# The tail of an attention and mixture-of-experts layer: first terms of the sums, additions and the last scaling placed elsewhere

## The chip, the cores and the metric

The kernel runs on one core of a Trainium2 chip. The metric is the device time of one execution in microseconds, from the first to the last instruction of the program with what lies around it. Without the profiler, three runs of the kernel before gave 538.71, 541.92 and 542.86 us; their median is 541.92 us. Its engines are named as in the profile: PE is TensorE's matmul, PEld its weight load, DVE is VectorE, ACT is ScalarE, POOL is GpSimd, SP is SyncE, which here only starts DMAs.

## The reference

The input x has 8 sequences of 512 tokens of 128 numbers, all float32. Two steps follow each other, each with a residual and a layer norm without scale and offset:

```python
x = _layernorm(x + attention(x))        # 16 heads of 8, causal, softmax
x = _layernorm(x + ffn(x))              # 14 experts, two for each token

# ffn, for one token:
#   w1, w2 = softmax of the token's logits, its two highest, made to sum to 1
#   out_k  = gelu(x @ W1[e_k] + b1[e_k]) @ W2[e_k] + b2[e_k]
#   result = clip(x + w1 * out_1 + w2 * out_2, -100, 100)

def _layernorm(x, eps=1e-05):
    m = mean(x); v = var(x)
    return (x - m) / sqrt(v + eps)
```

The part of the computation that this change touches is the very end: for each token the sum of x, its weighted biases and the two expert results, the clip, the residual, and the second layer norm.

## The kernel before

Tokens lie on 128 partitions. A sequence is four blocks of 128 tokens (`NQ` = 4), so a tensor for one sequence is 128 x 512 numbers; there are 8 sequences (`B`).

The kernel goes through these stages. Attention runs over 32 units (sequence and group of four heads) in a software pipeline written out by hand: a table of jobs gives each step its list of calls, so the order of instructions on each engine is the order in which the program issues them. Each engine works through its own list in order and waits on semaphores where an instruction needs another engine's result. While attention goes on, each finished sequence is routed: the two experts of each token are found, and GpSimd scatters the token's row, with its weight and its number, into the rows of those experts in a DRAM tensor, `XS`. Then the experts' blocks of 256 or 128 rows are loaded, multiplied through both layers, weighted, and scattered by GpSimd to `OS`, a DRAM tensor with two rows for each token (one for the first and one for the second expert). Between expert blocks, `biases(c)` (L1166) puts into `acc` what each token of sequence c has so far: its normalised input `y_sb` plus its weighted second-layer biases. `acc` and `z_sb` are the same memory as `x_sb`, the kernel's input, which is no longer needed.

The tail begins at L1242. It works sequence by sequence.

- `gather(c)` (L1245) starts two DMAs of 256 KB, one on SyncE's queue and one on ScalarE's, which bring the two expert rows of each token of sequence c back from `OS`. Six sequences are started at once; the buffers (`bufs=6`) of the first two are used again for sequences 6 and 7, as soon as TensorE has read them. The first gather waits for all scatters.
- `add_up(c)` (L1254) adds three terms in a PSUM bank by multiplying each with the identity matrix: first `acc`, then the two gathered tiles. The bank comes from the pool `ps_m`, which has two. The first sum's first term stands directly behind the last expert's matmuls in TensorE's queue; each later one stands behind the sum before it.
- `residual_2(c)` (L1260) clips the sum (L1263, VectorE, from PSUM to SBUF), adds `y_sb` (L1264, VectorE), and takes mean and variance of each of the four blocks (L220 and L221, VectorE, four pairs). `layernorm_scale` (L223) then gives scale and shift with four small GpSimd instructions: epsilon to the variance (L228), the power of -0.5 (L229), mean times scale (L230), and the sign (L231).
- `store(c)` (L1269) scales and shifts the four blocks with four ScalarE instructions (L1273) and starts one DMA of 256 KB to the output from SyncE's queue (L1281).

The loop at L1287 issues, for c from 0 to 9, `add_up(c)` and `residual_2(c)`, the gather six sequences ahead, and `store(c - 2)`. On VectorE the tail is thus, for each sequence in turn, one clip, one addition and four pairs of statistics instructions. Two other lines are named later because their instructions resemble new ones: L675, an addition of two 128 x 512 tiles by GpSimd in the attention part, and L770, a comparison on VectorE in the routing.

Of the kernel before, what the change touches and what calls it, by code (L numbers as in the profile page):

```python
# [8 lines left out]
FP = mybir.dt.float32  # L9
AF = mybir.ActivationFunctionType  # L10
ALU = mybir.AluOpType
# [4 lines left out]
P = 128  # L16
# [10 lines left out]
LN_EPS = 1e-5  # L27
# [9 lines left out]
def kernel(  # L37
# [18 lines left out]
    nc = tc.nc  # L56
    B, T, D = x.shape
    E, _, F = w1.shape
    NQ = T // P
# [28 lines left out]
    out_v = out.rearrange("b (t p) d -> p (b t) d", p=P)  # L88
# [8 lines left out]
    ident = const.tile([P, P], FP, tag="ident", name="ident")  # L97
# [61 lines left out]
    power = const.tile([P, NQ], FP, tag="power", name="power")  # L159
# [52 lines left out]
    y_sb = const.tile([P, NT, PW], FP, tag="y_sb", name="y_sb")  # L212
    nc.gpsimd.tensor_copy(y_sb[:, :, D + 1], ids[:, 0, :])
    stats = const.tile([P, NT, 2], FP, tag="stats", name="stats")
# [3 lines left out]
    def layernorm_stats(pool, src, t):  # L218
        st = pool.tile([P, nc.vector.BN_STATS_DIM], FP, tag="bn", name=f"bn_{t}", bufs=4)
        nc.vector.bn_stats(st, src)  # L220
        nc.vector.bn_aggr(stats[:, t, :], st)  # L221

    def layernorm_scale(pool, c, n):  # L223

        ts = slice(c * NQ, (c + 1) * NQ)
        rstd = pool.tile([P, NQ], FP, tag="rstd", name=f"rstd_{n}_{c}")
        shift = pool.tile([P, NQ], FP, tag="shift", name=f"shift_{n}_{c}")
        nc.gpsimd.tensor_scalar(rstd, stats[:, ts, 1], LN_EPS, 1.0, ALU.add, ALU.mult)  # L228
        nc.gpsimd.tensor_tensor(rstd, rstd, power, ALU.pow)  # L229
        nc.gpsimd.tensor_tensor(shift, stats[:, ts, 0], rstd, ALU.mult)  # L230
        nc.gpsimd.tensor_scalar(shift, shift, -1.0, 0.0, ALU.mult, ALU.add)  # L231
        return rstd, shift
# [23 lines left out]
    def after_scatters(inst, those):  # L256
        for s in those:
            tc.add_manual_dep(
                inst.ins,
                s.name,  # L260
                mybir.DependencyInfo(mybir.DependencyClass.Sync, mybir.DependencyReason.DATA),
                reason="reads what they wrote",
            )
# [9 lines left out]
    with tc.tile_pool(name="work", bufs=2) as work, tc.tile_pool(  # L273
        name="scratch", bufs=2, space=bass.MemoryType.DRAM
    ) as scratch, tc.tile_pool(
        name="ps_m", bufs=2, space=bass.MemoryType.PSUM
# [10 lines left out]
        def bank(name, dt=FP):  # L287
            return ps_m.tile([P, 2048 // mybir.dt.size(dt)], dt, tag="bank", name=name)
# [80 lines left out]
        def split(step, b, w, bias, nm):  # L369

            ps = bank(f"{nm}_{b}")
            nc.tensor.matmul(ps, w, xTs[b], start=True, stop=True)
            pc = work.tile([P, PC, T], BF, tag=f"{nm}pc", name=f"{nm}pc_{b}", bufs=1)
            nc.scalar.activation(pc[:, 0, :], ps, AF.Identity, bias=bias)
            rest = work.tile([P, T], FP, tag=f"{nm}rest", name=f"{nm}rest_{b}", bufs=1)
            nc.vector.scalar_tensor_tensor(
                rest, ps, bias, pc[:, 0, :], op0=ALU.add, op1=ALU.subtract
            )

            sc = scratch.tile([NG * HD, PC, GH, T], BF, tag=f"{nm}sc", name=f"{nm}sc_{b}")  # L380
            pieces[nm, b] = sc

            def store(cs):
                for c in cs:
                    nc.sync.dma_start(sc[:, c].rearrange("d j t -> d j t"), pc[:, c, :])

            def others():
                nc.scalar.copy(pc[:, 1, :], rest)
                nc.vector.tensor_tensor(pc[:, 2, :], rest, pc[:, 1, :], ALU.subtract)

            if step < 0:
                others()
                store(range(PC))
            else:
                at(step + 1, others)
                at(step + 1, store, (0,))
                at(step + 2, store, (1, 2))
# [104 lines left out]
        avs, pts, outs, sums = {}, {}, {}, {}  # L502
# [463 lines left out]
        def step_of(u, i):  # L966
            return u * UN + i
# [25 lines left out]
        for u in range(NU):  # L993
            b, g = divmod(u, NG)
            f, k = step_of(u, 0), step_of(u, 0) + LAG
# [148 lines left out]
        while s < NU * UN + LAG + 1 or s + 1 in jobs:  # L1144
# [5 lines left out]
            for fn, args in jobs.pop(s, ()):  # L1150
                fn(*args)
        held.close()
        ffn = held.enter_context(tc.tile_pool(name="ffn", bufs=3, reuse_waits="tile"))
# [3 lines left out]
                    name=n, bufs=2, space=bass.MemoryType.PSUM, reuse_waits="tile"  # L1157
# [6 lines left out]
        acc = z_sb = x_sb  # L1164
# [78 lines left out]
        got, sums, scales = {}, {}, {}  # L1243

        def gather(c):  # L1245
            got[c] = []
            for k, eng in enumerate((nc.sync, nc.scalar)):
                o = ffn.tile([P, NQ, D], FP, tag=f"o{k}", name=f"o{k}_{c}", bufs=6)
                inst = eng.dma_start(o, out_k[k][:, c * NQ : (c + 1) * NQ, :])
                if c == 0:  # L1250
                    after_scatters(inst, scatters["OS"])
                got[c].append(o)

        def add_up(c):  # L1254
            sums[c] = bank(f"sum_{c}").rearrange("p (t d) -> p t d", d=D)
            parts = acc[:, c * NQ : (c + 1) * NQ, :], *got.pop(c)
            for i, part in enumerate(parts):
                nc.tensor.matmul(sums[c], ident, part, start=(i == 0), stop=(i == 2))

        def residual_2(c):  # L1260
            ts = slice(c * NQ, (c + 1) * NQ)
            z = z_sb[:, ts, :]
            nc.vector.tensor_scalar(z, sums.pop(c), CLIP, -CLIP, ALU.min, ALU.max)  # L1263
            nc.vector.tensor_tensor(z, z, y_sb[:, ts, 0:D], ALU.add)  # L1264
            for i in range(NQ):
                layernorm_stats(ffn, z_sb[:, c * NQ + i, :], c * NQ + i)
            scales[c] = layernorm_scale(ffn, c, 1)

        def store(c):  # L1269
            rstd, shift = scales.pop(c)  # L1270
            for i in range(NQ):
                t = c * NQ + i
                nc.scalar.activation(  # L1273
                    z_sb[:, t, :],
                    z_sb[:, t, :],
                    AF.Identity,
                    bias=shift[:, i : i + 1],
                    scale=rstd[:, i : i + 1],
                )
            ts = slice(c * NQ, (c + 1) * NQ)  # L1280
            nc.sync.dma_start(out_v[:, ts, :], z_sb[:, ts, :])  # L1281

        inner.close()
        ffn = inner.enter_context(tc.tile_pool(name="tail", bufs=3, reuse_waits="tile"))
        for c in range(6):
            gather(c)
        for c in range(B + 2):  # L1287
            if c < B:
                add_up(c)
                residual_2(c)  # L1290
                if c + 6 < B:
                    gather(c + 6)
            if c >= 2:
                store(c - 2)


# [41 lines left out]
```

## Time and profile before

| What | Time |
|---|---|
| Median of three runs | 541.92 us |
| The profiled execution | 572.89 us |
| its span, from the first to the last instruction | 571.2 us |
| Last scatter's instruction ends on GpSimd | 530.6 us |
| First gathers start | 532.0 us |
| First sum complete, first clip starts | 539.6 us |
| Second clip starts | 542.9 us |
| Last statistics end | 564.2 us |
| Last scaling ends on ScalarE | 567.9 us |

Places in the profiled execution are given in microseconds from the start of its span; the profiled execution is slower than the runs, and a difference worked out in it is compared with its own time. In the timeline, a row is the start, the duration, the engine, the line in the code, the operation, the tile written and the tile read, and how often; in brackets stands how long the engine sat idle before, and what ended that. In the chain of waits, a row is the start, the share of time that the chain spends there, and the instruction. In a table by windows, each row has the window, its length, the busy time of PE, PEld, DVE, ACT and POOL with the number of instructions, then the granted TensorE clock (1.00 is full speed), the DMA engines' share and GB/s.

From 543 to 564 us VectorE is busy 19.59 of 21 us, TensorE 15.60, ScalarE 10.63 and GpSimd 11.15.

### The profile page before, as it was taken

The page shows a single profiled execution, that of the slowest core. Times are in us where ns is not written, and L with a number is a line of the kernel's source. Part 1 is how long each engine was busy: PE and PEld are TensorE (multiplying, and loading weights), DVE is VectorE, ACT ScalarE, POOL GpSimd, SP SyncE. Part 2 cuts the span into 40 slices and gives each one's busy share as a digit, 9 for nine tenths or more (in the row PEclk, how much of TensorE's full clock was granted, in tenths as well). Part 3 has the DMA queues.
Part 4 walks back from the last instruction along what each step waited for, and adds up shares of the span by engine and source line. Part 5 has one row for each costly group of instructions (what it writes and reads, how often), then busy time and mean ns, then how long its engine had stood idle before and what let it go on. Part 6 is the DMA issues. An engine that isn't in the chain of part 4 may idle for free.

```text
span 571.2 us, 10861 instructions
## 1 busy us (share of the span) xinstructions
PE 462.0 (81%) x3367; PEld 284.3 (50%) x3367; DVE 379.0 (66%) x932; ACT 307.5 (54%) x512; POOL 322.6 (56%) x678
## 2 busy tenths in 40 slices
PE   1757999999999899999999998777658787776491
PEld 0433655555555555445455554446546666665240
DVE  4239577779799798887888989517546344444194
ACT  0303677677677678658666474566224345444044
POOL 6001343545786785786876777636746545656153
PEclk9997799999999999999999999699669889989696
DMA  6153324434534535434344253322433212221763
GB/s 178 61 153 112 104 72 135 136 104 136 167 127 134 165 105 151 156 130 143 127 156 139 68 157 99 115 70 75 136 107 99 67 55 71 77 58 41 199 164 89
DMA packets 66739, 66.23 MB, mean 116 GB/s; under 512 B 10860, under 2 KB 55381, under 8 KB 66682
## 3 DMA queue, kind: packets, MB, share of 16 engines
q1 hardware_dynamic: 55008, 53.26, 31.3%
q0 software_dynamic: 4512, 8.47, 4.5%
q10 hardware_dynamic: 7162, 3.81, 2.5%
q8 instruction: 27, 0.44, 0.3%
q14 instruction: 30, 0.25, 0.2%
HBM read 37.75 MB, written 26.05 MB: 112 GB/s over the span
## 4 chain that ended last, share of the span: by engine, by line
PE 44%; DVE 21%; ACT 11%; issue 7%; DMA 6%; POOL 5%; another core or an unknown queue 3%; ACTq 1%; SPq 1%; DVEq 0%; POOLq 0%
PE av L587 10%; PE f L423 7%; PE b L509 6%; ACT pt L563 6%; PE h L1102 4%; PE o L1119 4%; PE f L433 2%; DVE ob L1127 2%; DVE mx L463 2%; DVE mx L468 2%; POOL pt L520 2%; PE bp L1177 2%; ACT oT L597 2%; DVE mx L475 2%
## 5 line engine op out<-in xcount | busy, mean ns | idle before, releaser
L563 ACT ACTIVATE pt<-b 128x1024 f32<-128x1024 f32 x160 | 162.8, 1021 | 44.7 <-PE b L509 30.6
L520 POOL TENSOR_SCALAR_AFFINE_SELECT pt<-pt 128x256 f32<-128x256 f32 (+1 forms) x210 | 91.6, 451 | 74.6 <-ACT pt L563 73.7
L423 PE MATMUL f<-ring 72*128 72x384 bf16 (+3 forms) x512 | 114.4, 307 | 17.8 <-DMA ring<-qsc 8.2
L243 POOL DMA_INDIRECT OS<-ob,bto_i x77 | 75.0, 974 | 62.4 <-DVE ob L1127 45.7
L509 PE MATMUL b<-ring 75*128 75x384 bf16 (+3 forms) x512 | 100.2, 307 | 6.8 <-ACT pt L563 3.4
L475 DVE TENSOR_REDUCE mx<-f 128x2 f32<-128x1024 f32 x64 | 78.1, 1223 | 29.1 <-PE f L433 27.1
L587 PE MATMUL av<-pt,v_aug 128*32 128x512 f32 (+3 forms) x1024 | 84.8, 443 | 4.8 <-POOL pt L520 4.2
L433 PE MATMUL f<-causal_bf,ident_bf 128*128 128x256 bf16 (+1 forms) x320 | 82.5, 258 | 0.0
L468 DVE TENSOR_REDUCE mx<-f 128x8 f32<-128x1024 f32 x64 | 77.1, 1214 | 5.6 <-PE f L433 5.3
L423 PEld LDWEIGHTS <-ring 72*128 72x128 bf16 x512 | 50.7, 100 | 52.1 <-issue 28.4
L1107 ACT ACTIVATE hT<-h,wt 128x256 f32<-128x256 f32 (+1 forms) x92 | 35.2, 436 | 61.6 <-PE h L1102 31.5
L509 PEld LDWEIGHTS <-ring 75*128 75x128 bf16 x512 | 42.4, 99 | 39.7 <-issue 27.5
L1119 PE MATMUL o<-wt,hT 128*128 128x128 f32 x308 | 48.0, 300 | 8.2 <-ACT hT L1107 7.5
L587 PEld LDWEIGHTS av<-pt,v_aug 128*32 128x32 f32 x1024 | 27.2, 109 | 51.9 <-issue 38.6
L1102 PE MATMUL h<-bxT,wt 128*128 128x256 f32 (+1 forms) x184 | 46.9, 382 | 6.9 <-ACT wt L1074 3.3
L1119 PEld LDWEIGHTS o<-wt,hT 128*128 128x128 f32 x308 | 45.3, 212 | 12.7 <-ACT hT L1107 9.1
L1127 DVE TENSOR_SCALAR ob<-o,bxb 128x128 f32<-128x128 f32 x77 | 24.1, 347 | 40.6 <-PE o L1119 14.7
L463 DVE TENSOR_REDUCE mx<-f 128x4 f32<-128x1024 f32 x32 | 39.1, 1223 | 16.0 <-PE f L433 11.8
L1102 PEld LDWEIGHTS h<-bxT,wt 128*128 128x128 f32 x184 | 33.0, 215 | 14.0 <-issue 6.7
L433 PEld LDWEIGHTS <-ident_bf 128*128 128x128 bf16 x320 | 31.7, 99 | 14.8 <-issue 2.3
L243 POOL DMA_INDIRECT XS<-y_sb,to_i x32 | 32.3, 1010 | 9.4 <-issue 5.6
L243 POOL DMA_INDIRECT XS<-second,to_i x32 | 32.4, 1012 | 8.9 <-issue 8.9
(215 smaller groups left out, 630.2 us busy)
## 6 DMA issues: line engine op xcount, KB each, us to landing
ring<-ksc SPq DMA_DIRECT2D x32, 288.0 KB
ring<-qsc SPq DMA_DIRECT2D x96, 96.0 KB
osc<-oT SPq DMA_DIRECT2D x24, 256.0 KB
bxb<-XS SPq DMA_DIRECT2D x31, 130.0 KB
ring<-in_L_ffn_w_dram SPq DMA_DIRECT2D x28, 128.0 KB
qsc<-qpc SPq DMA_DIRECT2D x24, 128.0 KB
ksc<-kpc SPq DMA_DIRECT2D x24, 128.0 KB
x_sb<-in_L_attn_x_dram SPq DMA_DIRECT2D x8, 256.0 KB
```

What stands on the lines that cost most here:

```text
L243: inst = nc.gpsimd.indirect_dma_start(dst, bass.IndirectOffsetOnAxis(ap=idx, axis=0), src, None, bounds_check=bound, oob_is_err=False,)
L423: nc.tensor.matmul(ps[:, col : col + W], qr[u % RING][0:KR, j, qb * P : (qb + 1) * P], kr[u % RING][0:KR, j, :W], start=first, stop=False, ...
L433: nc.tensor.matmul(out, ident_bf, causal_bf[:, 0:n, :], start=False, stop=True, skip_group_check=True,)
L463: nc.vector.reduce_max(mx[:, :, 5], ps.rearrange("p b (s k) -> p (b s) k", s=2), axis=AX.X)
L468: nc.vector.reduce_max(mx[:, j : j + 2, 1:5], ps.rearrange("p b (s k) -> p b s k", k=P), axis=AX.X,)
L475: nc.vector.reduce_max(mx[:, j : j + 2, 7], ps, axis=AX.X)
L509: nc.tensor.matmul(ps[:, col : col + W], kr[u % RING][:, j, kb * P : (kb + 1) * P], qr[u % RING][:, j, kb * P :], start=first, stop=True, ...
L520: nc.gpsimd.affine_select(out=view, in_=view, pattern=[[0, k] for k in n] + [[1, P]], compare_op=ALU.is_ge, fill=0.0, base=0, channel_mult ...
L563: nc.scalar.activation(pt, ps, AF.Exp, scale=SCALE)
L587: nc.tensor.matmul(avs[u][HS * j : HS * (j + 1), kb * P :], v_aug[b % 2][:, kb, g * GH + j, :], p, start=(kb == 0), stop=(kb == 2),)
L1102: nc.tensor.matmul(hp[:, f, :], wt[:, f * P : (f + 1) * P], xT, start=True, stop=True)
L1119: nc.tensor.matmul(op[:, s, :], hT[:, f, s * P : (s + 1) * P], wt[:, F + f * D : F + (f + 1) * D], start=(f == 0), stop=(f == NFC - 1),)
```

## The change

The tail's functions are taken apart and issued in another order, and some of their work is given to other engines.

- The first terms of the sums (`begin_sum`) are issued apart from the other two (`add_up`). They go into a pool of their own, `ps_t`, with six PSUM banks. Six first terms are issued with the first six gathers. Those of sequences 6 and 7 follow the clips of sequences 0 and 1, whose banks they use again; in TensorE's queue they stand ahead of the remaining terms of sequences 1 and 2.
- The addition of `y_sb` is GpSimd's for sequences 0 to 6, and VectorE's for the last one.
- Epsilon is added to the variance by VectorE. GpSimd takes only the power. The shift (minus mean times scale) is one VectorE instruction.
- The order on VectorE is: clip of c, shift of c-2, statistics of c-1, variance plus epsilon of c-1. The last sequence's addition and statistics stand ahead of the shift of the seventh.
- For the last sequence, two blocks are scaled by VectorE and stored from SyncE's queue, and two are scaled by ScalarE and stored from ScalarE's queue.

```diff
+        def begin_sum(c):
+            sums[c] = ps_t.tile([P, NQ, D], FP, tag="sum", name=f"sum_{c}")
+            nc.tensor.matmul(
+                sums[c], ident, acc[:, c * NQ : (c + 1) * NQ, :], start=True, stop=False
+            )
+
         def add_up(c):
-            sums[c] = bank(f"sum_{c}").rearrange("p (t d) -> p t d", d=D)
-            parts = acc[:, c * NQ : (c + 1) * NQ, :], *got.pop(c)
-            for i, part in enumerate(parts):
-                nc.tensor.matmul(sums[c], ident, part, start=(i == 0), stop=(i == 2))
+            for i, part in enumerate(got.pop(c)):
+                nc.tensor.matmul(sums[c], ident, part, start=False, stop=(i == 1))
 
-        def residual_2(c):
+        def clip(c):
             ts = slice(c * NQ, (c + 1) * NQ)
             z = z_sb[:, ts, :]
             nc.vector.tensor_scalar(z, sums.pop(c), CLIP, -CLIP, ALU.min, ALU.max)
-            nc.vector.tensor_tensor(z, z, y_sb[:, ts, 0:D], ALU.add)
+
+            if c < B - 1:
+                nc.gpsimd.tensor_tensor(z, z, y_sb[:, ts, 0:D], ALU.add)
+
+        def measure(c):
+            ts = slice(c * NQ, (c + 1) * NQ)
+            if c == B - 1:
+                z = z_sb[:, ts, :]
+                nc.vector.tensor_tensor(z, z, y_sb[:, ts, 0:D], ALU.add)
             for i in range(NQ):
                 layernorm_stats(ffn, z_sb[:, c * NQ + i, :], c * NQ + i)
-            scales[c] = layernorm_scale(ffn, c, 1)
+            rstd = ffn.tile([P, NQ], FP, tag="rstd", name=f"rstd_1_{c}")
+            nc.vector.tensor_scalar(
+                rstd, stats[:, ts, 1], LN_EPS, 1.0, ALU.add, ALU.mult
+            )
+            nc.gpsimd.tensor_tensor(rstd, rstd, power, ALU.pow)
+            scales[c] = rstd
+
+        def move(c):
+            ts = slice(c * NQ, (c + 1) * NQ)
+            shift = ffn.tile([P, NQ], FP, tag="shift", name=f"shift_1_{c}")
+            nc.vector.scalar_tensor_tensor(
+                shift, stats[:, ts, 0], -1.0, scales[c], op0=ALU.mult, op1=ALU.mult
+            )
+            scales[c] = scales[c], shift
 
         def store(c):
             rstd, shift = scales.pop(c)
...
+            for half, eng in enumerate((nc.sync, nc.scalar)):
+                for i in range(2 * half, 2 * half + 2):
+                    t = c * NQ + i
+                    z = z_sb[:, t, :]
+                    if c == B - 1 and half == 0:
+                        nc.vector.tensor_scalar(
+                            z, z, rstd[:, i : i + 1], shift[:, i : i + 1], ALU.mult, ALU.add
+                        )
+                    else:
+                        nc.scalar.activation(
...
+                if c == B - 1:
+                    ts = slice(c * NQ + 2 * half, c * NQ + 2 * half + 2)
+                    eng.dma_start(out_v[:, ts, :], z_sb[:, ts, :])
+            if c < B - 1:
+                ts = slice(c * NQ, (c + 1) * NQ)
+                nc.sync.dma_start(out_v[:, ts, :], z_sb[:, ts, :])
 
         inner.close()
         ffn = inner.enter_context(tc.tile_pool(name="tail", bufs=3, reuse_waits="tile"))
+        ps_t = inner.enter_context(
+            tc.tile_pool(
+                name="ps_t", bufs=6, space=bass.MemoryType.PSUM, reuse_waits="tile"
+            )
+        )
+
         for c in range(6):
             gather(c)
+            begin_sum(c)
         for c in range(B + 2):
             if c < B:
                 add_up(c)
-                residual_2(c)
+                clip(c)
                 if c + 6 < B:
                     gather(c + 6)
-            if c >= 2:
+                    begin_sum(c + 6)
+            if c == B:
+                measure(c - 1)
+            if c > 1:
+                move(c - 2)
                 store(c - 2)
+            if 1 <= c < B:
+                measure(c - 1)
```

More of the change, by code (lines that the diff above doesn't have):

```diff
@@ L1269, in store @@
+        def move(c):
[5 more added lines that the diff above has]
+            scales[c] = scales[c], shift
         def store(c):
             rstd, shift = scales.pop(c)
[L1271 to L1279, printed above, removed]
@@ L1280, in store @@
-            ts = slice(c * NQ, (c + 1) * NQ)
-            nc.sync.dma_start(out_v[:, ts, :], z_sb[:, ts, :])
+            for half, eng in enumerate((nc.sync, nc.scalar)):
[8 more added lines that the diff above has]
+                        nc.scalar.activation(
+                            z,
+                            z,
+                            AF.Identity,
+                            bias=shift[:, i : i + 1],
+                            scale=rstd[:, i : i + 1],
+                        )
+                if c == B - 1:
+                    ts = slice(c * NQ + 2 * half, c * NQ + 2 * half + 2)
+                    eng.dma_start(out_v[:, ts, :], z_sb[:, ts, :])
@@ L1283 @@
+            if c < B - 1:
+                ts = slice(c * NQ, (c + 1) * NQ)
+                nc.sync.dma_start(out_v[:, ts, :], z_sb[:, ts, :])
         inner.close()
         ffn = inner.enter_context(tc.tile_pool(name="tail", bufs=3, reuse_waits="tile"))
+        ps_t = inner.enter_context(
+            tc.tile_pool(
+                name="ps_t", bufs=6, space=bass.MemoryType.PSUM, reuse_waits="tile"
+            )
+        )
         for c in range(6):
             gather(c)
+            begin_sum(c)
```

## The prediction

> **What bounds the kernel now.** The change touches only what follows the last expert block, so I read the chain of waits in order of time from there.
>
> ```profile
> 531.98 3.76 DMA o<-OS
> 535.78 7.12 PE sum L1258 x10
> 542.92 0.70 DVE x_sb L1263
> ...
> 543.65 0.70 DVE x_sb L1264
> ...
> 564.68 1.02 POOL rstd L229
> ```
>
> The tail is in three parts: the first gather is awaited until 535.78 us; TensorE adds up the first sums, at half clock, until 542.9; then VectorE alone sets the pace. Its chain repeats every 3.03 us (clip at 546.07 and at 549.10) to the last sequence. TensorE, ScalarE and GpSimd wait beside it: ScalarE sat idle 29.6 us before its scalings, behind GpSimd's shift. Next, the timeline of the same stretch, for the hand-over to GpSimd and the end.
>
> ```profile
> 543.25 1.04 POOL L229 TENSOR_TENSOR rstd<-rstd,power 128x4 f32<-128x4 f32 x1
> 543.65 0.69 DVE L1264 TENSOR_TENSOR x_sb<-x_sb,y_sb 128x512 f32<-128x512 f32 x1
> ...
> 564.06 0.18 DVE L221 BATCH_NORM_AGGREGATE stats<-bn 128x2 f32<-128x6 f32 x1
> 564.40 0.19 POOL L228 TENSOR_SCALAR rstd<-stats 128x4 f32<-128x4 f32 x1 [1.19 <-DVE stats L221]
> ...
> 566.27 1.65 ACT L1273 ACTIVATE x_sb<-x_sb,shift,rstd 128x128 f32<-128x128 f32 x4 [1.38 <-POOL shift L231]
> ```
>
> A power costs GpSimd 1.01 to 1.04 us for four columns. Now it lies beside VectorE's next sequence, and nothing on VectorE waits for it: shift and its sign are GpSimd's too. ScalarE ends at 567.92; the last store and the end of the program take until 571.2, another 3.28.
>
> **What moves off VectorE.** The addition of y, 0.69 us (0.72 to the next start), leaves VectorE for seven of eight sequences. Two small instructions come: the variance with epsilon (nearest row L944, 176 ns) and the shift, a scalar_tensor_tensor on four columns (nearest L782, 162 ns); each delays its successor by about 0.10. If nothing waited, a round would be 0.60 (clip) + 0.10 + 1.51 (first bn to last aggregate, 544.37 to 545.88) + 0.20 + 0.10 = 2.51 us instead of 3.03.
>
> **The wait that comes in.** The order on VectorE becomes: clip of c, shift of c-2, statistics of c-1, variance of c-1. The shift reads the power, and the power starts only when the variance, the instruction just before the clip, is done. Only the clip covers it. From the variance's start (call it R): 0.17 for itself, 0.10 to GpSimd, 1.01 for the power, 0.03 back, so the shift starts at R+1.31; the clip frees VectorE at R+0.70. VectorE stands 0.6 us each round, with the statistics of the next sequence queued behind the shift, and ScalarE behind these. Round: 1.31 + 0.17 - 0.08 (a successor starts that much before the end) + 1.51 + 0.20 = 3.11 us. That alone eats the whole gain. The 0.10 lies between 0.08 (149.51 to 149.59 below) and 0.16 (564.24 to 564.40).
>
> **What the moved addition does.** GpSimd's queue becomes: power of c-2, addition of c, power of c-1. The clip of c is done by R+0.8, so the addition of c is ready to go when the power ends. The trace of before has this addition's like (x plus bias) and the two hand-overs:
>
> ```profile
> 149.10 0.20 POOL L787 TENSOR_SCALAR w<-gap 128x4 f32<-128x4 f32 x1
> 149.33 0.18 DVE L788 RECIPROCAL w<-w 128x4 f32<-128x4 f32 x1 [1.34 <-POOL w L787]
> 149.59 0.20 POOL L789 TENSOR_TENSOR w<-gap,w 128x4 f32<-128x4 f32 x1 [0.30 <-DVE w L788]
> 149.73 0.19 POOL L790 COPY y_sb<-w 128x4 f32<-128x4 f32 x1
> ...
> 333.94 1.27 POOL L675 TENSOR_TENSOR xb<-x_sb,bo_bc 128x512 f32<-128x512 f32 x1
> 333.98 1.31 DVE L770 TENSOR_TENSOR hot<-rank,best 128x56 f32<-128x56 f32 x1
> ```
>
> VectorE starts 0.03 after GpSimd's result (149.30 to 149.33). A GpSimd instruction that needs nothing of the one before starts 0.06 before that one's end (149.73 against 149.79). So the addition starts 0.09 ahead of the shift. And L770, which takes 0.22 us elsewhere, took 1.31 when it started 0.04 behind such an addition, and ended 0.08 after it. It reads two operands from SBUF; so does the shift (mean and rstd). L817, also two operands, lasts 0.36 instead of 0.27 each time it starts 0.14 behind a short GpSimd product. The Trainium skill ("SBUF — State Buffer", section "SBUF: two separate sides") says why: VectorE and GpSimd share a pair of ports under an exclusive lock; a VectorE instruction with two SBUF inputs and a GpSimd instruction exclude each other for the whole instruction. The power rows above speak against the "whole": L1264, with two inputs, ran its usual 0.69 in the middle of a power. By the rule the powers would also block; by the rows only an instruction that streams many columns does. I follow the rows: the additions block, the powers do not. The shift of c-2 is then held to the end of the addition of c:
>
> R + 0.17 + 0.10 + 1.01 - 0.06 + 1.27 + 0.08 = R+2.57, then -0.08 + 1.51 + 0.20: a round of 4.20 us.
>
> Bounds: no hold, 3.11; hold, 4.20. L770 and the shift differ in columns (56 against 4), but the wait is for the other engine, so I take the hold. The statistics read one operand, and an L477 reduction under L675 took its usual 0.17; they are counted as free of it.
>
> **The first sums.** Six first terms run in the wait, 6 x 0.86 from 525.7, to about 530.9 us (their banks are free once the last expert outputs are evacuated, about 526.4). They take one 0.86 off each sum, but VectorE is the bound after the second sum, and the first sum had its first term early already. Could they keep TensorE's clock up? Windows of 3.41 us on the grid at which the clock changes:
>
> ```profile
> 462.43:465.84 3.41, 0.91 (x9) 0.67 (x7) 0.85 (x5) 1.76 (x4) 1.73 (x3) 1.00 0.33 99
> 465.84:469.26 3.42, 3.21 (x6) 1.90 (x7) 1.22 (x5) 0.00 (x0) 1.91 (x2) 0.50 0.25 77
> ...
> 534.11:537.53 3.42, 1.75 (x2) 0.84 (x3) 0.00 (x0) 0.00 (x0) 0.00 (x0) 0.50 1.14 315
> 537.53:540.94 3.41, 3.41 (x5) 1.35 (x4) 1.31 (x2) 0.00 (x0) 0.00 (x0) 0.50 1.20 291
> ```
>
> The first number after the window's length is TensorE's busy time, the third from the end the granted clock. The Trainium skill ("TensorE: Matmul & The Clock Gate", Part 1) drops the clock after an idle window of about 3.4 us. 530.9 to 535.78 is 4.9 us idle, which holds a whole window in (4.9-3.41)/3.41 = 44% of phases; in the rest the sum would be ready near 537.5 and 2.1 us would be won. But the row of 462.43 lost the clock with 0.91 us of work in its window, and 4.9 us of idle time leave no more than 0.96 in the worse of two windows. I take the clock as lost, and the first sum where it is, 539.6.
>
> The second sum gets later: the seventh first term reuses the first bank and stands ahead of it in TensorE's queue, waiting for the first clip. 539.60 + 0.69 + about 1.1 (partly half clock) + 1.72 puts the second clip at about T = 543.2, against 542.92: +0.3. Before, VectorE used that wait for the first statistics; now these stand behind the second clip.
>
> **The sum.** First variance R0 = T + 0.60 + 1.51 + 0.20 = T+2.31. The third clip waits for the eighth first term (again behind a clip) and its own two terms: T+3.3. It ends after the first power, so this addition comes late and the shift passes ahead of it: R1 = T + 3.32 + 0.60 + 0.09 + 1.71 = T+5.72. Four rounds with the hold: R5 = T+22.52. The last sequence has no GpSimd addition, so one round without: R6 = T+25.63. Then VectorE's own addition and statistics, 0.09 + 0.72 + 1.71: R7 = T+28.15. The seventh sequence's shift stands behind that, so ScalarE scales it from R7+0.29 to R7+1.94 and only then the last two blocks, to R7+2.72. VectorE's half is ready at about R7+2.1 (L904 gives 0.33 and 0.23 more), hidden. From there the 3.28 of before, and an estimated 0.1 for two stores of the same moment: T+34.25 = 577.45. Before: 571.2. That is +6.3 us; the profiled execution would be 572.89 + 6.3 = 579.2. It is longer than the median of the runs by 31 us, but the tail's steps are fixed latencies, so I carry the difference over whole: 541.92 + 6.3 = 548.2.
>
> What is hidden: GpSimd's work (2.28 us a sequence against 1.6, inside the round) and the stores of the first six sequences. The end itself is 0.8 shorter (6.94 to 6.1 after the last variance), counted above.
>
> **Rivals.** (1) The shift gets its operands before the addition takes the ports: 4 x 1.09 less, +1.9, 543.8. For it: L770 is one instance. Against: the start order, and L817's five. (2) Not slower: the power comes back before the clip ends, and the round is 2.51. After R1 five such rounds give R6 = T+18.3 and the end at T+26.9, 1.1 us ahead of before: 540.8. It needs the power and its hand-overs within 0.5 us; all rows say 1.0. (3) Worse: the third round is held too (+1.1), or single-operand statistics are slowed by additions: 550 and above. For it: the third clip's margin is only about 0.4 us.
>
> **Chances.** Forecast 0.60, (1) 0.25, (2) 0.08, (3) 0.07. One per cent, 5.4 us, is about what a measurement of this kernel can tell from no change (its three runs span 4.2). The forecast lies 0.9 us above that bound, so about 0.7 of its chance is on the slower side: 0.52 slower with (3), 0.45 within, 0.03 faster. Range 542.5 (leaves out most of (2)) to 551 (takes in the extra held round).
>
> **What would show it.** Shifts of four columns lasting 1.1 to 1.3 us on VectorE in rounds 3 to 6, each ending with a GpSimd addition; the clip to clip distance 4.2 there; TensorE at half clock at 536; ScalarE's seventh sequence directly ahead of the eighth. Wrong, if shifts last 0.2 with 0.6 us of idle time before them, if the distance is below 3.0, or if the first sum is ready by 538.

## The result

The changed kernel takes 546.86 us (median of six runs, 545.29 to 549.45) against 539.09 for the kernel before (six runs in all, 535.61 to 542.86): the ratio is 1.0157, with a 95% interval of 1.012 to 1.0194. The change makes the kernel about 8 us slower.

The two profiled executions can't be compared from end to end. The first one of the kernel before stood some 30 us longer in the expert stage, ahead of the tail: its first gathers start at 531.98 us, those of the changed kernel at 495.97. A second profile of the kernel before (below) has them at 497.94. So I compare tails, from the start of the first gather to the end of the span:

| | before | changed | difference |
|---|---|---|---|
| first gather to first clip | 7.62 us | 7.56 us | -0.06 |
| first clip to second clip | 3.32 us | 5.38 us | +2.06 |
| second clip to the last variance (before: to where L221's last result could be read) | 21.34 us | 28.49 us | +7.15 |
| from there to the end | 6.94 us | 6.10 us | -0.84 |
| sum | 39.22 us | 47.53 us | +8.31 |

The chain of waits of the changed kernel, in order of time (start, share of time, instruction):

```profile
499.71 3.80 PE sum L1262 x4
...
503.53 0.70 DVE x_sb L1267
...
504.28 2.08 PE sum L1256 x2
506.35 2.53 PE sum L1262 x4
...
508.91 0.70 DVE x_sb L1267
...
515.18 1.03 POOL rstd L1283
516.21 0.02 issue
516.23 1.13 DVE shift L1289
...
519.25 1.03 POOL rstd L1283
520.28 0.02 issue
520.30 1.15 DVE shift L1289
```

Two things are new in it. Between the first and the second clip, TensorE's seventh first term (L1256) stands in the chain, behind the first clip. And in each round from 515 us on, GpSimd's power and VectorE's four-column shift stand in it, which were beside it before. The timeline of the changed kernel shows why a shift of four columns takes over a microsecond:

```profile
515.18 1.02 POOL L1283 TENSOR_TENSOR rstd<-rstd,power 128x4 f32<-128x4 f32 x1 [0.70 <-DVE rstd L1280]
516.17 1.17 POOL L1270 TENSOR_TENSOR x_sb<-x_sb,y_sb 128x512 f32<-128x512 f32 x1
516.23 1.13 DVE L1289 SCALAR_TENSOR_TENSOR shift<-stats,rstd 128x4 f32<-128x4 f32 x1 [0.54 <-POOL rstd L1283]
...
532.93 0.16 DVE L1289 SCALAR_TENSOR_TENSOR shift<-stats,rstd 128x4 f32<-128x4 f32 x1 [0.60 <-POOL rstd L1283]
...
534.88 0.69 DVE L1276 TENSOR_TENSOR x_sb<-x_sb,y_sb 128x512 f32<-128x512 f32 x1
535.12 1.31 POOL L1283 TENSOR_TENSOR rstd<-rstd,power 128x4 f32<-128x4 f32 x1 [2.22 <-DVE rstd L1280]
```

GpSimd's addition starts at 516.17, 0.06 us ahead of the shift, and the shift ends at 517.36, 0.02 after it. VectorE stood idle 0.54 for the power before that. Where no addition follows the power (532.93), the shift takes 0.16. Four shifts are held; the clips of their rounds and the next one start at 515.01, 519.08, 523.23, 527.43 and 531.64, 4.07 to 4.21 us apart.

### The profile page after: what moved, and what is told of

It is laid out like the page before. It is cut to its first block, busy times and chain, and to the rows that moved or that the text cites. A ratio compares the mean times of both kernels' runs of the same rounds, so it can differ in the third digit from the quotient of the medians.

```text
span 543.5 us, 10853 instructions
## 1 busy us (share of the span) xinstructions
PE 448.6 (83%) x3367; PEld 276.0 (51%) x3367; DVE 382.3 (70%) x943; ACT 306.0 (56%) x510; POOL 325.8 (60%) x661
## 4 chain that ended last, share of the span: by engine, by line
PE 49%; DVE 17%; ACT 12%; DMA 7%; POOL 6%; issue 6%; ACTq 1%; SPq 1%; DVEq 0%; POOLq 0%
PE av L587 12%; PE f L423 8%; PE b L509 7%; ACT pt L563 7%; PE o L1119 5%; PE h L1102 4%; PE f L433 3%; POOL pt L520 2%; DVE mx L468 2%; DVE mx L463 2%; ACT oT L597 2%; DMA OS<-ob,bto_i 2%; PE bp L1177 2%; ACT x_sb L1305 2%; DVE ob L1127 2%
## 5 line engine op out<-in xcount | busy, mean ns | idle before, releaser
L1102 PE MATMUL h<-bxT,wt 128*128 128x256 f32 (+1 forms) x184 | 43.7, 361 | 5.6 <-DVE begins L873 3.3
L1119 PE MATMUL o<-wt,hT 128*128 128x128 f32 x308 | 43.5, 282 | 1.3 <-ACT hT L1107 1.3
L1119 PEld LDWEIGHTS o<-wt,hT 128*128 128x128 f32 x308 | 41.7, 197 | 4.2 <-ACT hT L1107 2.1
L1102 PEld LDWEIGHTS h<-bxT,wt 128*128 128x128 f32 x184 | 30.4, 198 | 11.1 <-ACT wt L1074 5.4
```

Source lines behind the costliest of these rows:

```text
L1102: nc.tensor.matmul(hp[:, f, :], wt[:, f * P : (f + 1) * P], xT, start=True, stop=True)
L1119: nc.tensor.matmul(op[:, s, :], hT[:, f, s * P : (s + 1) * P], wt[:, F + f * D : F + (f + 1) * D], start=(f == 0), stop=(f == NFC - 1),)
```

## The experiments

All tails below are from one profile each, from the start of the first gather to the end; ratios are to the kernel before on the same chip. They are worked out from the single runs of both, and differ by up to 0.24% from the quotient of the two medians.

| Run | tail, us | median, us | before, us | ratio, 95% interval |
|---|---|---|---|---|
| kernel before, twice | 39.2, 39.4 | | | |
| changed, twice | 47.5, 48.4 | 546.9, 548.8 | 539.1, 540.7 | 1.0157 (1.012 to 1.0194), 1.0128 (1.0055 to 1.0202) |
| the addition waits for the shift | 43.9 | 548.3 | 539.6 | 1.0175 (1.0124 to 1.0226) |
| additions on VectorE | 42.6 | 544.3 | 539.6 | 1.0111 (1.0053 to 1.0169) |
| later first terms | 45.1 | 546.4 | 539.6 | 1.0135 (1.0085 to 1.0184) |
| quarter addition | 45.2 | 547.1 | 539.6 | 1.0150 (1.0104 to 1.0196) |
| first terms alone | 40.5 | 543.1 | 540.7 | 1.0044 (1.0021 to 1.0068) |
| before, clock kept | 37.5 | 538.1 | 540.7 | 0.9947 (0.9920 to 0.9974) |
| changed, clock kept | 44.3 | 544.3 | 538.0 | 1.0117 (1.0070 to 1.0163) |
| changed, both mended | 40.4 | 539.5 | 538.0 | 1.0034 (1.0014 to 1.0053) |
| clip by two engines | 35.5 | 536.7 | 540.7 | 0.9912 (0.9887 to 0.9937) |
| clip by two, second form | 32.9 | 532.0 | 538.0 | 0.9882 (0.9839 to 0.9924) |

### The changed kernel once more

> The changed kernel once more, as the measure for the runs beside it. The profiles give 47.5 us from the first gather's start to the end for it, 39.2 for the kernel before: 8.3 us more. If the shorter tails of the four runs before this one are the whole difference, this one is the slowest of all against the kernel before, by 8 us (547.5); if something ahead of the tail differs between executions and chips, the difference lies anywhere between 6 and 11 us while the tail in the profile is again 47.5.

The tail of this second profile is 48.4 us, four shifts are held for 1.13 us, and the first two clips (506.41 and 512.23) are 5.82 apart. The medians differ by 8.1 us. Both losses, the held shifts and the late second sum, are thus in both profiles of the changed kernel.

### The held shift: one wait more

```diff
-            if c < B - 1:
-                nc.gpsimd.tensor_tensor(z, z, y_sb[:, ts, 0:D], ALU.add)   # in clip(c)
...
             if c > 1:
                 move(c - 2)
+            if c < B - 1:
+                add_y(c, moved.get(c - 2))   # the addition, with a wait for that shift
+            if c > 1:
                 store(c - 2)
```

`add_y` (not shown) is the same addition, which also waits for the shift that it is given.

> The changed kernel with one wait more: GpSimd's addition of sequence c also waits for VectorE's shift of sequence c-2, so it can no longer start ahead of it; nothing else moves. If the additions hold the shifts (forecast's theory), the four shifts of 1.13 us last 0.16 again, the rounds shrink from 4.2 to 3.1 us, and the kernel gains 4 x 1.09 = 4.4 us: about 542.5, and 43 us from the first gather's start to the end instead of 47.5. If the shift is long for a reason of its own (the power's result arriving late, a slow form of instruction), the rounds stay at 4.2 or grow and the time stays at 546.9 or above.

All eight shifts last 0.15 or 0.16 us, the rounds from the fourth clip on are 3.10 to 3.24, and the tail is 43.9 us, 3.6 less than the changed kernel's. A wait was added and the tail got shorter, so the shift's length is the addition's doing. The time without a profile didn't follow: the profiled execution took 543.45 us, the three others 547.4 to 550.1; 542.5 was expected. The pair with the clock kept, below, repeats the test.

### The held shift: dose and response

```diff
-                nc.gpsimd.tensor_tensor(z, z, y_sb[:, ts, 0:D], ALU.add)
+                nc.gpsimd.tensor_tensor(
+                    z[:, 0:1, :], z[:, 0:1, :], y_sb[:, c * NQ : c * NQ + 1, 0:D], ALU.add
+                )
```

> The changed kernel with GpSimd's additions cut to the first of the four blocks of a sequence (the residual is left out for the other three blocks of sequences 0 to 6). Dose and response: if the shift is held exactly as long as the addition runs, an addition of about 0.4 us gives shifts of 0.35 to 0.4 us instead of 1.13, rounds of 3.35 and 3.5 us less in all: 543.4. If the hold is a fixed cost of two engines meeting, the shifts stay near 1.1 us.

The timeline of this run, at the first held shift:

```profile
516.99 1.02 POOL L1285 TENSOR_TENSOR rstd<-rstd,power 128x4 f32<-128x4 f32 x1 [1.42 <-DVE rstd L1282]
517.99 0.45 POOL L1270 TENSOR_TENSOR x_sb<-x_sb,y_sb 128x128 f32<-128x128 f32 x1
518.04 0.41 DVE L1291 SCALAR_TENSOR_TENSOR shift<-stats,rstd 128x4 f32<-128x4 f32 x1 [0.54 <-POOL rstd L1285]
```

An addition of 0.45 us gives a shift of 0.41; all four are 0.41. The hold lasts as long as the addition. Each held shift is 0.72 shorter, which makes 2.9 us; the expected 3.5 was too large. The tail is 2.4 us shorter than the changed kernel's, because in this profile the first clip comes 0.26 us later after the first gather (7.82) and the second 0.19 later after the first (5.57). My 0.35 to 0.4 for the shift was near. The median is 547.1 us and not 543.4: here too the time without a profile didn't follow.

### The additions back on VectorE

```diff
-            if c < B - 1:
-                nc.gpsimd.tensor_tensor(z, z, y_sb[:, ts, 0:D], ALU.add)
+            nc.vector.tensor_tensor(z, z, y_sb[:, ts, 0:D], ALU.add)
...
```

> The changed kernel with the additions of y back on VectorE, directly behind the clips; all the rest as changed. Forecast's theory: no addition on GpSimd, so no hold; clip and addition together (1.3 us) now cover the power's round trip (1.31 us), so the 0.6 us of waiting goes as well and is replaced by the 0.7 us of the addition: rounds of 3.2 us, about 543, 43.5 us of tail. If the waiting for the power were the whole loss and no hold existed, moving the addition back would win nothing: 547.

The rounds are 3.20 to 3.28 us, the shifts 0.15 to 0.16 with no idle time before them: clip and addition cover the power's way to GpSimd and back. The tail is 42.6 us. VectorE does more work than in the changed kernel and is done sooner. Part of the 5 us by which the tail is shorter than the changed kernel's is the clock: here the second clip came 3.63 after the first. The median is 544.3 us; 543 was expected.

### The late second sum: the seventh first term moved

```diff
                 if c + 6 < B:
                     gather(c + 6)
-                    begin_sum(c + 6)
+                if 3 <= c < 5:
+                    begin_sum(c + 3)
```

> The changed kernel with the first terms of sequences 6 and 7 issued three and three sequences later, so that no first term that waits for a clip stands ahead of the second and third sum in TensorE's queue. Theory: the second sum was late (5.4 us after the first, 3.3 before the change) because TensorE stood idle for the clip and so stayed at half clock for another window. Then the second clip comes about 3 us sooner, 2.2 to 2.5 us after the first; but the third clip is then early too, so the shift of the first sequence is held by an addition as the others are (+0.8): together about -2.4, 544.5, tail 45. If the half clock has nothing to do with the wait, only the wait and the matmuls go, about 0.8 + 0.9 us, and with the added hold the time stays within 1 us of 546.9.

The second clip starts 2.07 us behind the first (506.99 and 509.06), and the first sequence's shift is now held too, 1.15 us. The tail is 45.1, as expected. So the seventh first term, its wait for the first clip and what they do to the clock made the second sum late; the half clock's part is the next test. The median is 546.4 us, where 544.5 was expected: no faster than the changed kernel, as far as the noise lets one tell.

### The late second sum: half clock

TensorE's windows in the changed kernel, on the grid at which the clock changes (length, busy time of PE, and near the end the granted clock):

```profile
497.69:501.11 3.42, 1.40 (x2) 0.84 (x3) 0.00 (x0) 0.00 (x0) 0.00 (x0) 0.50 1.08 300
501.11:504.52 3.41, 2.63 (x4) 0.58 (x3) 0.69 (x1) 0.00 (x0) 0.21 (x1) 0.50 1.19 291
504.52:507.93 3.41, 3.41 (x5) 1.35 (x6) 0.00 (x0) 0.00 (x0) 0.96 (x1) 0.51 1.20 290
507.93:511.35 3.42, 2.64 (x7) 0.98 (x6) 2.27 (x10) 0.00 (x0) 1.18 (x1) 1.00 1.17 287
```

(The clock changes about 0.1 us ahead of the edges shown, which leaves the 2.63 as it is.) The second of these windows is busy for 2.63 us of 3.41; the other 0.78 is the wait for the first clip. The clock stayed at half for one window more, and most of the first term and of the second sum ran in it.

Where the windows fall differs from one execution to the next. Six profiles have this opening without further matmuls. In four (the changed kernel twice, the run with the wait, the quarter addition) the whole wait lay inside one window, which was busy for 2.63 or 2.64 us, and the second clip came 5.38 to 5.82 us after the first. In the run with the additions on VectorE the clock was back at 503.65, ahead of the wait; in the run with the first terms alone (below) it came back at 504.85, in the middle of the wait, after a window that was busy for 2.70 us. In these two the second clip came 3.63 and 3.62 after the first. So the loss is frequent, but not certain.

To test the half clock, six matmuls into an unused bank follow the first terms, so that the clock is still full when the gathers land:

```diff
         for c in range(6):
             gather(c)
             begin_sum(c)
+        idle = bank("idle").rearrange("p (t d) -> p t d", d=D)
+        for i in range(6):
+            nc.tensor.matmul(idle, ident, acc[:, 0:NQ, :], start=True, stop=True)
```

> The changed kernel with six matmuls into an unused bank behind the six first terms, so that TensorE is busy until shortly before the first gathers land. Theory: the second sum's delay (5.4 to 5.8 us behind the first instead of the 3.6 that were forecast) is half clock kept up by the wait for the first clip. At full clock it comes 3.3 us behind the first, and the first about 1.5 to 2 us sooner: tail 47.5 - 2.1 - 1.5 = 43.9, about 4 us less than the changed kernel, 544. The four held shifts of 1.13 us stay. If the delay is the wait for the clip itself, only the first sum comes sooner: tail 46.

The timeline of this run:

```profile
503.77 0.69 DVE L1267 TENSOR_SCALAR x_sb<-sum 128x512 f32<-128x512 f32 x1 [11.72 <-PE sum L1262]
...
504.52 1.12 PE L1256 MATMUL sum<-x_sb,ident 128*128 128x512 f32 x2 [0.78 <-DVE x_sb L1267]
...
505.48 1.88 PE L1262 MATMUL sum<-o,ident 128*128 128x512 f32 x4
...
507.40 0.69 DVE L1267 TENSOR_SCALAR x_sb<-sum 128x512 f32<-128x512 f32 x1 [2.94 <-PE sum L1262]
```

Clip to clip is 3.63 us (3.3 expected); the first clip comes 6.09 us after the first gather's start instead of 7.56. Both come sooner at full clock, with the wait for the clip still there, so the half clock was the larger part of the delay; the tail is 44.3 (43.9 expected). The 3.6 that I had forecast for the changed kernel is the distance at full clock.

### Both mended

The same six matmuls, and the additions wait for the shifts.

> The changed kernel with the clock kept as in the run beside it, and with the additions waiting for the shifts, so that both costs are away: no shift over 0.2 us, rounds of 3.1 to 3.2. The tail is 43.9 - 3.6 = 40.3, 3.6 us less than beside it, about 540. If the time without a profile doesn't follow the tail (as in the run with the wait alone), it stays at 544.

```profile
512.03 1.02 POOL L1280 TENSOR_TENSOR rstd<-rstd,power 128x4 f32<-128x4 f32 x1 [0.63 <-DVE rstd L1277]
513.08 0.16 DVE L1294 SCALAR_TENSOR_TENSOR shift<-stats,rstd 128x4 f32<-128x4 f32 x1 [0.54 <-POOL rstd L1280]
...
513.32 1.18 POOL L1285 TENSOR_TENSOR x_sb<-x_sb,y_sb 128x512 f32<-128x512 f32 x1 [0.27 <-DVE shift L1294]
```

Now the shift goes first and the addition follows it. The tail is 40.4 us, 3.9 less than with the hold, and here the runs follow: 539.5 against 544.3, 4.8 less on the same chip. So the hold costs about 4 us of the kernel's time. The fair comparison is with the kernel before with its clock kept too (37.5, below): 2.9 us are left. The first two clip distances are 3.63 and 3.62 us instead of 3.13 and 3.03, with a first term's wait for a clip in each: 1.1 us. From the fourth clip on the rounds are 3.10 to 3.24 instead of 3.03: the 0.54 to 0.6 us of waiting for the power in each eats what the addition's leaving gave. (One short distance, 2.48 from the third to the fourth clip, makes up for most of this.) And 1.8 us lie behind the last clip, where the new order has one sequence more to measure.

### First terms alone

The kernel before with the first part of the change (`begin_sum` and its six banks), nothing else.

> The kernel before with only the first part of the change: the first terms apart, in six banks, those of sequences 6 and 7 behind the first two clips. The additions, the scale and shift, and the stores are as before. Theory: nothing is won in the wait for the gathers, since the clock is lost all the same; the second sum comes about 2 us later behind the first clip (5.4 us after the first instead of 3.3), and VectorE, which sets the pace, starts its second sequence 2.0 to 2.3 us later: 541.5, tail 41.5 us. Rival: first terms done early shorten the sums, TensorE is ahead, and the tail stays at 39 us or falls to 37.

The tail of its profile is 40.5 us, 1.2 more than before; its first two clips are 3.62 us apart, since the clock rose earlier there (0.79 of full speed from 504 to 506 us). The runs give 2.4 us more (1.0044), about what was expected. In neither is anything won.

### The kernel before again, and with the clock kept

> The kernel before once more, for a second profile: the first one stood 30 us longer in the expert stage than its runs without a profile. If that has nothing to do with the tail, the span is near 539 us here, and the tail from the first gather's start to the end is again 39.2 us, a little more or less with the clock's windows (half clock over the first sums).

Span 537.3 us, tail 39.4, first two clips 3.46 apart: the tail of the first profile was the usual one.

```diff
         for c in range(6):
             gather(c)
+        idle = bank("idle").rearrange("p (t d) -> p t d", d=D)
+        for i in range(9):
+            nc.tensor.matmul(idle, ident, acc[:, 0:NQ, :], start=True, stop=True)
```

> The kernel before with nine matmuls into an unused bank while the first gathers are on their way (7.7 us of work in the 9 us gap), to keep TensorE at full clock. Their result is used nowhere. If the half clock is what delays the first sums, the first sum is ready 1.9 to 2.1 us sooner and the second no longer delays VectorE (3.03 us after the first): 2.3 us less, 537, tail 36.9 us. If the first sums wait for the gathers' data instead, nothing changes: 539.3.

The clips of the first two sequences in this run:

```profile
504.84 0.69 DVE L1263 TENSOR_SCALAR x_sb<-sum 128x512 f32<-128x512 f32 x1 [12.68 <-PE sum L1258]
...
507.97 0.66 DVE L1263 TENSOR_SCALAR x_sb<-sum 128x512 f32<-128x512 f32 x1
```

They are 3.13 us apart, VectorE no longer waits for the second sum, and the first clip comes 6.12 us after the first gather's start. The tail is 37.5, 1.7 to 1.9 less; the kernel gains 0.5%. Nine useless matmuls make it faster, six useful ones did not: with the nine TensorE worked on until 500.3 and stood 2.53 us before the gathered rows came, with the first terms alone it stopped at 494.1 and stood 6.28 us.

### A version that beats both

```diff
-            nc.vector.tensor_scalar(z, sums.pop(c), CLIP, -CLIP, ALU.min, ALU.max)
-            nc.vector.tensor_tensor(z, z, y_sb[:, ts, 0:D], ALU.add)
+            nc.scalar.activation(z, sums.pop(c), AF.Relu, bias=plus)      # plus = 100
+            nc.vector.scalar_tensor_tensor(
+                z, z, 2.0 * CLIP, y_sb[:, ts, 0:D], op0=ALU.min, op1=ALU.add
+            )                                                             # y - 100, by ScalarE before the gathers
```

with the nine matmuls and the change's split of the last sequence.

> A version meant to beat both, built on the kernel before: the clip is taken apart into relu(sum + 100) on ScalarE, which also moves the sum out of PSUM, and min with 200 plus (y - 100) in one VectorE instruction; ScalarE takes the 100 off y while the gathers are on their way; TensorE's clock is kept as in the run beside it; the last sequence's scaling and store are split as in the change. VectorE's round is then 0.72 + 1.61 = 2.33 us instead of 3.03, ScalarE's about 0.65 + 1.65 = 2.3 with small gaps: about 2.4. Eight rounds save 5 us, the clock 2.3, the split end 0.8, the first relu costs 0.7: 7.4 less, 532, tail about 32 us. If ScalarE becomes the bound because each relu waits behind a whole scaling, rounds stay near 3.0 and only 2.4 us are won: 537.

The rounds are 2.30 to 2.46 us, as worked out, but the tail is 35.5 and not 32, and the median 536.7 and not 532. The timeline says why:

```profile
498.87 9.95 ACTq L1249 DMA_DIRECT2D o<-OS  x6
...
508.86 0.69 ACT L1263 ACTIVATE x_sb<-sum,plus 128x512 f32<-128x512 f32 x1 [11.80 <-DMA o<-OS]
```

ScalarE starts its sixth gather only at about 508.8 us, since that start waits for an earlier transfer, and the first relu stands behind it in ScalarE's queue. In the kernel before, ScalarE's first scaling starts 13 us after the first gather, so nothing had been held there. The nine matmuls did not keep the clock in this profile: TensorE stood 2.61 us, and from 504 to 506 us the granted clock was 0.50. In the second form only three of the eight gathers are in that queue, and eleven matmuls keep the clock:

```diff
-            for k, eng in enumerate((nc.sync, nc.scalar)):
+            for k, eng in enumerate((nc.sync, nc.scalar if c < 3 else nc.sync)):
```

> The version with the clip on two engines, with eleven instead of nine matmuls to keep the clock, and only three gathers in ScalarE's queue (the others in SyncE's). In its first form ScalarE's first relu stood behind the start of its sixth gather until 10 us after the first gather's start, and VectorE began at 10.7 us. If that was the cause, VectorE begins at 6.8 us, the rounds stay 2.34 us, and the tail is 31.6 us instead of 35.5: about 533. If SyncE's queue alone moves the gathers more slowly, VectorE waits for later sums and part of that is lost: 535.

```profile
510.88 0.69 ACT L1263 ACTIVATE x_sb<-sum,plus 128x512 f32<-128x512 f32 x1 [0.31 <-PE sum L1258]
...
511.60 0.69 DVE L1264 SCALAR_TENSOR_TENSOR x_sb<-x_sb,y_sb 128x512 f32<-128x512 f32 x1 [0.15 <-ACT x_sb L1263]
...
514.17 0.69 DVE L1264 SCALAR_TENSOR_TENSOR x_sb<-x_sb,y_sb 128x512 f32<-128x512 f32 x1 [0.16 <-ACT x_sb L1263]
```

VectorE begins 6.6 us after the first gather's start instead of 10.7, and the tail is 32.9 us; the kernel takes 532.0 us, 1.2% less than before. Most of the 4.1 us by which VectorE begins sooner is the queue, since in the first form the first sum was ready at about 505.4 and relu started at 508.86. The rounds are 2.57 us: relu waits for the sum. Three terms at 0.86 us are 2.58, so TensorE is the bound now. Here, for the first time, first terms taken out of the rounds might be worth something. That was not tried.

## Why the prediction was right

The direction, the sizes of the rounds and the range were right: 548.2 was forecast, in a range of 542.5 to 551, and 546.86 measured. That the time came so near is in part luck: the sum started from 541.92, while the kernel before came out at 539.09 in six runs, and this error hides most of one in the other direction, the second sum. The difference is the better test: +6.3 forecast, +8.3 in the tails, +7.8 in the medians.

- **The hold.** Forecast: the addition starts 0.09 us ahead of the shift and holds it to its end, in four rounds of 4.20 us. Measured: 0.06 ahead, shifts of 1.13, rounds of 4.07 to 4.21. The wait, the quarter addition and the mended pair show it as the cause. The first of the rivals, the shift passing ahead, fell. That the rounds met 4.20 has a little luck in it: the addition took 1.17 and not 1.27, so the first held round is 4.07, and two hand-overs that grow from the fourth sequence on (next point) bring the later ones back to 4.21. The forecast weighed the Trainium skill's "whole instruction" ("SBUF — State Buffer", section "SBUF: two separate sides") against the power rows, and it came out as the rows had it: an addition holds as long as it runs (1.17 and 1.13, 0.45 and 0.41), while in the run with the additions on VectorE a two-operand addition that started at 514.76, inside a power (514.22, 1.01), took its usual 0.69.
- **The uncovered power.** Forecast 0.6 us of idle time on VectorE each round; measured 0.54 to 0.60. A round without a hold was forecast at 3.11 and took 3.23 (variances at 531.57 and 534.80). The forecast left out that from the fourth sequence on a semaphore instruction stands ahead of the variance and of the power, where the three buffers of `rstd` come round (the link to the buffers was not tested): from the last aggregate to the variance it is 0.29 us instead of 0.21, from there to the power 0.32 instead of 0.25. In the run with both mended the rounds grow in the same way, from 3.10 to 3.24. The second rival, a power that comes back before the clip ends, fell.
- **The third round.** Forecast: the third clip comes after the first power, so this shift escapes. Measured: clip at 512.53 (3.62 after the second, 3.3 forecast), shift 0.15 at 513.14, addition only at 513.30. With the third clip sooner behind the second it doesn't escape, as the run with later first terms shows (2.40 us behind; shift 1.15).
- **The second sum: the term that was mis-sized.** "+0.3" was forecast for the second clip, with the seventh first term at "about 1.1 (partly half clock)" and the second sum at full clock. Measured +2.06. The wait for the clip was in the sum, but not that this wait can leave a hole in TensorE's window and so put the return of the full clock off by one more window, as in four of six profiles. At full clock the distance is 3.63, the forecast's 3.6. (The forecast also has the sums of before at half clock until 542.9; its trace has the full clock from about 540.9 on.)
- **The first sum.** Forecast: the clock is lost in spite of the first terms. It was, and the first clip's place did not move (7.62 and 7.56). In this profile the gap was 5.9 us rather than the 4.9 worked out and held a whole idle window, so it does not decide between the rows and the Trainium skill's rule of one idle window ("TensorE: Matmul & The Clock Gate", Part 1). Two other traces side with the rows: the clock fell after a window (3.41 us) that was still busy for 1.29 us with the additions on VectorE, and for 1.15 us in the first form of the clip by two.
- **From the second clip to the last variance** 28.15 was forecast and 28.49 measured (the third clip 0.3 later, the held rounds 0.16 shorter in sum, the last two rounds 0.2 longer); **the end** was forecast at 6.1 and is 6.10.

What stays open is the time of the runs with the wait alone, the quarter addition and the later first terms: their tails were 2.4 to 3.6 us shorter than the changed kernel's in the profile, while their medians (548.3, 547.1 and 546.4) lie about the changed kernel's own (546.9 and 548.8). No trace of the other executions exists. The clock's windows fall differently in each execution, and with the clock kept the times lie closer together (536.2 to 540.0 in 14 runs of the kernel before with the clock kept, 536.9 to 544.9 in 39 of 41 runs of the kernel before beside it, the other two at 545.7 and 547.8), which points to these windows. And the tail's start varies: but for the first one, the profiles have the first gather between 495.65 and 499.14 us, a spread as large as these gains. Neither was shown to be the reason.

## What to carry to other kernels

Before work is moved from VectorE to GpSimd, look at what is next in each of the two queues when a result passes from GpSimd to VectorE: here GpSimd's next instruction started 0.06 us sooner than VectorE's consumer, and the consumer, with two SBUF operands, then waited for all of it (1.13 us). An instruction that is four columns wide cost its round trip through the other engine (1.3 us from variance to shift), not its work (0.16), and what covers that round trip must be counted before the cover (here the addition itself) is taken away. Starting terms early won nothing here, where their engine was not the bound; what it left in that engine's queue ahead of the next result cost more than it saved (2.4 us with the first terms alone).

## What the runs showed that was not expected

- The hold works in the other direction as well. The seventh power, which started at 535.12 while VectorE's two-operand addition ran (534.88 to 535.57), took 1.31 us instead of 1.02. In the second form of the clip by two, GpSimd's epsilon (L228), 0.19 elsewhere, took 0.74 where it started together with VectorE's L1264 (0.69, at 514.17). In the before kernel the powers start ahead of that instruction, and none is longer than 1.04.
- A window of 3.41 us with 2.63 or 2.64 us of TensorE work (77%) did not bring the full clock back in four profiles; one with 2.70 us (79%) did in the run with the first terms alone, and one with 3.21 us in the kernel before (465.84 us).
- GpSimd's addition of two whole tiles took 1.17 us here, against 1.27 for L675 in the attention stage.
